# A transformer block on one core: the attention division is put ahead of the residual on VectorE, and the second norm's square root goes one slot later

## The chip, the cores and the metric

The kernel runs on one core of one Trainium2 chip. The metric is device time in microseconds (us): the median over runs of the whole program. All numbers of the profile come from one further execution, taken with the hardware profiler.

Five engines work side by side, each on its own list of instructions and strictly in the order of that list: TensorE (PE in the profile, its weight loads PEld), VectorE (DVE), ScalarE (ACT), GpSimd (POOL) and SyncE (SP), which here only issues DMA transfers. Engines wait for each other through semaphores.

## The reference

The input `x` is 4 sequences of 1024 tokens with 512 features, in float32; `t` is a condition vector for each sequence. What is computed:

```python
def _tc_rmsnorm(x, t, gw, gb, bw, bb):
    g = (t @ gw.T + gb)[:, None, :]
    b = (t @ bw.T + bb)[:, None, :]
    inv_rms = jax.lax.rsqrt(jnp.mean(x * x, axis=-1, keepdims=True) + EPS)
    return g * x * inv_rms + b

def _swiglu(x, gate_w, hid_w, out_w):
    return jax.nn.silu(x @ gate_w.T) * (x @ hid_w.T) @ out_w.T

def block(x, t, ...):
    x = x + attention(_tc_rmsnorm(x, t, g1w, g1b, b1w, b1b), Wq, Wk, Wv, Wo)
    return x + _swiglu(_tc_rmsnorm(x, t, g2w, g2b, b2w, b2b), gate_w, hid_w, out_w)

out = x + block(x, t, ...)
```

The attention has 16 heads of 32 features and a full softmax; the hidden size of the feed-forward part is 2048.

## The kernel before

**Tiling.** The 4096 tokens are 8 query blocks of 512 tokens (`n`). Activations lie transposed, features on the 128 partitions and tokens along the free axis. For each block, attention runs over 4 groups of 4 heads and 2 halves of 256 queries: 8 softmax jobs `j` for a block, 64 in all. A job takes 4 rounds `r`, each over 256 keys, so there are 256 rounds.

**Slots.** One loop, `while g < END`, runs a software pipeline over slots `g`, one round to a slot. The order on PE, DVE and ACT is the order in which the loop writes the instructions (`manual_schedule`); SP is ordered by the framework. In slot `g` the kernel computes the scores of round `g` (`scores`, L316, PE), copies them to SBUF (`keep`, L323, ACT) and takes them into the running maximum (`running_max`, L328, DVE); it adds the shift to round `g-5` (`shifted`, L369, DVE) and exponentiates it (`exponential`, L372, ACT); and it multiplies round `g-6` with the values (`weighted`, L382, PE). The exponential of one slot is therefore the operand of the `weighted` of the next. `kind = g % 4` tells the slots apart: in kind 0 the maximum of a finished job is transposed and split, and its sums are taken (`take_sums`); in kind 1 the shift is spread over the partitions (`parts_T`, `spread`) and `take_av` copies the finished product. Below, "slot 16" means the 16th slot of a block, `g % 32 == 16`; "third slots" are those with kind 2.

**Division.** `inverse` (L422, RECIPROCAL) and `normalize` (L431, a product) on DVE turn a job's product into attention output `oT`. They stand near the end of a kind 0 or a kind 2 slot: before slot `FS` = 60 in kind 2 (except for the last job of a block); from then on in kind 0, except for the jobs whose slot group starts at 12, 24 or 28 of a block, which go to kind 2, that is, to slots 14, 26 and 30.

**Feed-forward filler.** From slot 60 on, PE's free time is filled with the feed-forward part of the block before: one of 16 hidden tiles `p` for every two slots. The products `pa` and `pb` (L112) lie in PSUM. In an even slot: `pair_26`, `copy_156` (L545, ACT), `filler` (the contraction `pc` of an earlier tile with `ow`, 32 matmul records), `pair_7`, `sub_5` (L552, DVE, reads what `pair_7` wrote). The residual, `take_contract` (L583, DVE), adds `pc` to `res` and so sets the PSUM buffer of `pc` free. In an odd slot: `pair_3`, `gate_tanh` (L562, ACT), `pair_15` of the next tile, `take_5` (L526, ACT), `gate` (L567, DVE), `add_15` (L530, DVE), `pair_4`, `hidden` (L570, DVE). `pc` and `pa` share two PSUM buffers of the pool `ps`: the `pa` that `pair_15` opens in a kind 3 slot takes the buffer of the `pc` of the kind 2 slot ahead of it. Its first matmul (`pa<-x,fa`) waits for that residual.

**Second norm.** The scale of the feed-forward norm is made in small steps that are hung on the ends of slots (`after(g, ...)`; such work follows everything else in its slot): mean (`norm_mean`), `norm_compact` and `take` bring the 512 sums as a 128x4 tile `few` through DRAM, `root` (L173, ACT, a square root), `invert` (L177, DVE), `put` (L182, a DMA to DRAM) and `norm_spread` (L188, a DMA back, broadcast to 128 partitions). `norm_scale` (L199, DVE) then uses it. There are 7 of these chains in the loop, for blocks 0 to 6. `e` is `g0` for block 0 and `g0 - 4` for the others, where `g0 = (n + 1) * 32`.

**ACT's function tables.** The square root and the exponential need different tables; ahead of `root`, and again ahead of the next exponential, ACT gets an ACT_TABLE_LOAD (L173 and L372). Copies and the tanh need none of their own.

The even slots and the end of a slot before, where the change works (shortened):

```python
                one, two, evict = filler(p)
                one()
                two()
                if g < NR:
                    running_max(g, 0)
                    running_max(g, 1)
                if evict is not None:
                    evict()
                pair_7(p)
                sub_5(p)
```

Of the kernel before, what the change touches and what calls it, by code (L numbers as in the profile page):

```python
# [24 lines left out]
def tile_cond_transformer_block(  # L25
# [299 lines left out]
    def running_max(r: int, k: int):  # L325
        j, u = divmod(r, UN)
        if u:
            nc.vector.tensor_tensor(rmax[j], rmax[j], raw[r][:, k, :, :], ALU.max)  # L328
        elif k:
            rmax[j] = sb.tile([P, HG, HQ], F32, tag="rmax", name=f"rmax{j}")  # L330
            nc.vector.tensor_tensor(rmax[j], raw[r][:, 0, :, :], raw[r][:, 1, :, :], ALU.max)
# [74 lines left out]
    def take_av(j: int):  # L406
        avs[j] = sb.tile([P, HQ], F32, tag="avs", name=f"avs{j}", bufs=2)
        nc.scalar.copy(avs[j], av.pop(j))
# [12 lines left out]
    def inverse(j: int):  # L421
        nc.vector.reciprocal(state["total", j], state["total", j])  # L422
# [166 lines left out]
    GB = C * (NB // HQ)  # L589
    BS = GB * UN  # L590
# [15 lines left out]
    def after(g, fn, *a):  # L606
        ended.setdefault(g, []).append((fn, a))
# [21 lines left out]
    for b in range(1, B):  # L629
        for half in range(QB):  # L630
            s = math.ceil((len(queue) + 1) / PACE)
            s4 = s - 4 - (s - 6) % UN
            tag = f"a{b}_{half}"
# [10 lines left out]
    FS = BS + 28  # L644
# [3 lines left out]
    for n in range(NBLK):  # L648
        g0 = (n + 1) * BS
        pin(g0 + 6, load_res, n)  # L650
        e = g0 if n == 0 else g0 - 4
        go = e + 13 if n < NBLK - 1 else g0 + 8
        for d in range(C):
            first.append((go, None, project_out, (n, d)))
            pin(go - 3 + (d // 2 * 4 if n else 0), load_wo, n, d)
        if n < NBLK - 1:
            tag = f"f{n}"
            after(e + 16, add_res, n)
            for k in range(2):
                after(e + 15 + k, lambda n=n, tag=tag, k=k: norm_squares(x2[n], tag, k))  # L660
            if n == 0:
                between(e + 17, norm_mean, tag, False)
            else:
                amid.setdefault(e + 17, []).append((norm_mean, (tag, True)))
            after(e + 17, norm_compact, tag)
            after(e + 19, take, tag)
            after(e + 20, root, tag)
            after(e + (20 if n == 0 else 21), invert, tag)
            after(e + (21 if n == 0 else 22), put, tag)
            after(e + (22 if n == 0 else 24), norm_spread, tag)  # L670
            scales, mods = ((24, 24, 25, 25), (25, 25, 26, 26)) if n == 0 else ((22, 22, 24, 24), (23, 23, 25, 25))
            for c in range(C):
                after(g0 + scales[c], lambda n=n, tag=tag, c=c: norm_scale(x2[n], tag, c))
                between(g0 + mods[c], lambda n=n, c=c: norm_mod(1, n // QB, x2[n], c))
            for i in range(4):
                after(g0 + (26, 26, 27, 28)[i] - (n > 0 and i == 0), token_sums, n, i)
# [27 lines left out]
    with tc.manual_schedule(  # L704
# [69 lines left out]
        while g < END:  # L774
            kind = g % UN
            r_x, r_v = g - UN - 1, g - UN - 2
            x_on, v_on = 0 <= r_x < NR, 0 <= r_v < NR
            j_m = g // UN - 1
            m_on = 0 <= j_m < NR // UN
            j_s = g // UN - 2  # L780
            s_on = 0 <= j_s < NR // UN
            j_n = g // UN - 3
            n_on = 0 <= j_n < NR // UN
            ffn = g >= FS
            p = (g - FS) // 2
            even = g % 2 == 0
            columns[0] = DH

            if kind == 1 and m_on:
                parts_T(j_m)  # L790
            if g < NR:
                scores(g)
            if kind == 1 and m_on:
                spread(j_m, 0)
            if kind == 0 and n_on:
                fold_sum(j_n)
            if kind == 1 and j_n == GB + 1:
                normalize(GB)
            if x_on and kind != 1:
                shifted(r_x)  # L800
            if late is not None:
                late()
                late = None
            for fn, a in pinned.pop(g, []):
                fn(*a)
            if v_on:
                weighted(r_v)
                accumulate(r_v)
            if kind == 1 and m_on:
                spread(j_m, 2)  # L810
                mT.pop(j_m)
                shifted(r_x, slice(0, HG // 2))
                shifted(r_x, slice(HG // 2, HG))
            if g < NR:
                keep(g)
            if kind == 1 and s_on:
                take_av(j_s)
            due = bool(first) and first[0][0] <= g
            if not ffn:
                if x_on:  # L820
                    exponential(r_x)
                evict = chain(g, FG)
                if kind == 0:
                    take_sums(j_n)
# [3 lines that stand above are left out]
                if kind == 0 and m_on:  # L828
                    columns[0] = P
                    max_T(j_m)  # L830
                    parts(j_m)
                if evict is not None:
                    evict()
                for fn, a in halfway.pop(g, []):
                    fn(*a)
                if g == FS - 1:
                    columns[0] = DH
                    pair_15(0)
                    take_5(0)
                    add_15(0)  # L840
                elif even:
                    late = chain(g, FG)
                if g in (FS - 4, FS - 2):
                    load_f((g - FS + 4) // 2)
            elif even:
                load_f(p + 2)
                pair_26(p)
                copy_156(p)
                if kind == 0:
                    take_sums(j_n)  # L850
                if x_on:
                    exponential(r_x)
                if kind == 0 and m_on:
                    max_T(j_m)
                    parts(j_m)
# [3 lines that stand above are left out]
                if g < NR:  # L859
                    running_max(g, 0)  # L860
                    running_max(g, 1)
                if evict is not None:
                    evict()
                pair_7(p)
                sub_5(p)
                for fn, a in halfway.pop(g, []):
                    fn(*a)
            else:
                extra = due or len(queue) > FG
                evict = None  # L870
                if kind == 3 and extra:
                    evict = chain(g)
                pair_3(p)
                if kind == 3:
                    gate_tanh(p)
                if x_on:
                    exponential(r_x)
                pair_15(p + 1)
                take_5(p + 1)
                for fn, a in amid.pop(g, []):  # L880
                    fn(*a)
                if kind == 1:
                    gate_tanh(p)
                    if extra:
                        spare_bank[0] = True
                        evict = chain(g)
                if g < NR:
                    running_max(g, 0)
                if kind == 3 and evict is not None:
                    evict()  # L890
                if kind == 3:
                    gate(p)
                if g < NR:
                    running_max(g, 1)
                add_15(p + 1)
                if kind == 1:
                    gate(p)
                    if evict is not None:
                        evict()
                pair_4(p)  # L900
                hidden(p)
                if due:
                    chain(g)()
                for fn, a in halfway.pop(g, []):
                    fn(*a)
            if n_on and j_n < direct and kind in (0, 2):


                at = g - kind
                in_first = j_n % GB == GB - 1 or (at >= FS and at % BS not in (12, 24, 28))  # L910
                if in_first == (kind == 0):
                    inverse(j_n)

                    if j_n != GB:
                        normalize(j_n)
            columns[0] = DH
            for fn, a in ended.pop(g, []):
                fn(*a)
            if g == FS + 2 * FG - 2:
                load_ow(0)  # L920
            g += 1
# [90 lines left out]
```

## Time and profile before

| what | value |
|---|---|
| median of 3 runs | 2450.79 us (2449.7 to 2451.94) |
| the profiled execution | 2455.29 us, of which its span 2453.4 us |
| PE busy | 2385.5 us (97% of the span) |
| DVE busy | 1940.7 us (79%) |
| ACT busy | 1413.2 us (58%) |
| POOL busy | 172.4 us (7%) |
| mean granted TensorE clock | 0.994 |
| RECIPROCAL 128x256 (L422), 64 of them | 1744 ns each |
| product `oT` (L431), 64 | 425 ns |
| residual (L583), 128 | 689 ns |
| `sub_5` (L552), 128 | 430 ns |
| table load (L173, L372) | 1283 ns |

"Busy" is the time in which an engine had an instruction of the program running. The starts of records on one engine can lie closer together than their durations, since a next instruction may begin while the last one drains; for PE the ends are modelled. Where "waited for" is given, the profile infers the releaser from semaphore events. A time such as "974.22" is us from the start of the span. A slot is measured here from its first score matmul (L316) to that of the next.

### The profile page before, as it was taken

The page shows a single profiled execution, that of the slowest core. Times are in us where ns is not written, and L with a number is a line of the kernel's source. Part 1 is how long each engine was busy: PE and PEld are TensorE (multiplying, and loading weights), DVE is VectorE, ACT ScalarE, POOL GpSimd, SP SyncE. Part 2 cuts the span into 40 slices and gives each one's busy share as a digit, 9 for nine tenths or more (in the row PEclk, how much of TensorE's full clock was granted, in tenths as well). Part 3 has the DMA queues.
Part 4 walks back from the last instruction along what each step waited for, and adds up shares of the span by engine and source line. Part 5 has one row for each costly group of instructions (what it writes and reads, how often), then busy time and mean ns, then how long its engine had stood idle before and what let it go on. Part 6 is the DMA issues. An engine that isn't in the chain of part 4 may idle for free. (4 is left out here: it accounts for less than half of the span.)

```text
span 2453.4 us, 72677 instructions
## 1 busy us (share of the span) xinstructions
PE 2385.5 (97%) x32553; PEld 1135.9 (46%) x32553; DVE 1940.7 (79%) x2183; ACT 1413.2 (58%) x1495; POOL 172.4 (7%) x207
## 2 busy tenths in 40 slices
PE   8999999999999999999999999999999999999999
PEld 3333334344444544544454544454445445444444
DVE  2688888878799988998899979997999799843332
ACT  3677776765566656665566656665666566512110
POOL 0000000000000000000000000000000000000000
PEclk9999999999999999999999999999999999999999
DMA  6599999988788788889888888898788888853442
GB/s 216 166 304 259 256 258 240 231 202 219 198 205 210 188 226 209 208 207 229 204 200 213 225 197 209 204 230 207 198 207 203 224 200 204 198 165 117 140 131 70
DMA packets 185988, 501.79 MB, mean 205 GB/s; under 512 B 21319, under 2 KB 78663, under 8 KB 158286
## 3 DMA queue, kind: packets, MB, share of 16 engines
q0 software_dynamic: 28656, 208.68, 43.9%
q1 hardware_dynamic: 156734, 288.47, 35.4%
q8 instruction: 256, 4.19, 0.7%
q14 instruction: 54, 0.44, 0.1%
q10 hardware_dynamic: 288, 0.01, 0.0%
HBM read 246.44 MB, written 41.97 MB: 118 GB/s over the span
## 5 line engine op out<-in xcount | busy, mean ns | idle before, releaser
L369 DVE TENSOR_TENSOR raw<-raw,shift 128x2048 f32<-128x2048 f32 (+1 forms) x320 | 588.8, 1857 | 25.6 <-ACT shift L364 25.6
L323 ACT COPY raw<-sc 128x2048 f32<-128x2048 f32 x256 | 479.7, 1874 | 187.4 <-PE sc L316 130.8
L372 ACT ACTIVATE raw<-raw 128x2048 f32<-128x2048 f32 x256 | 490.8, 1917 | 157.1 <-DVE raw L369 154.8
L328 DVE TENSOR_TENSOR rmax<-rmax,raw 128x1024 f32<-128x1024 f32 x384 | 469.5, 1223 | 48.8 <-ACT raw L323 42.2
L112 PE MATMUL pc<-h,ow 128*32 128x512 f32 x4096 | 470.5, 596 | 5.2 <-DMA ow<-in_out_w 4.2
L382 PE MATMUL av<-raw,v 128*32 128x256 f32 x4096 | 271.9, 383 | 35.6 <-ACT raw L372 35.1
L396 POOL DMA_DIRECT2D raw<-raw x192 | 165.3, 861 | 1967.4 <-ACT raw L372 878.9
L316 PE MATMUL sc<-q,k 32*128 32x256 f32 x4096 | 293.3, 400 | 1.0 <-ACT raw L323 1.0
L112 PE MATMUL pa<-x,fa 128*32 128x256 f32 x4096 | 272.5, 384 | 4.1 <-DVE pa L530 4.1
L112 PE MATMUL pa<-sums,fw 128*32 128x256 f32 x4096 | 271.5, 383 | 0.0
L112 PEld LDWEIGHTS pc<-h,ow 128*32 128x32 f32 x4096 | 128.6, 110 | 250.7 <-issue 231.9
L316 PEld LDWEIGHTS sc<-q,k 32*128 32x128 f32 x4096 | 184.9, 184 | 117.4 <-issue 75.8
L112 PE MATMUL pkq<-y,wkq 128*32 128x512 f32 (+1 forms) x1664 | 232.5, 594 | 4.3 <-ACT y L202 4.1
L112 PEld LDWEIGHTS pa<-x,fa 128*32 128x32 f32 x4096 | 124.7, 110 | 119.7 <-DVE pa L530 21.4
L382 PEld LDWEIGHTS av<-raw,v 128*32 128x32 f32 x4096 | 110.4, 109 | 149.4 <-ACT raw L372 66.0
L112 PEld LDWEIGHTS pa<-sums,fw 128*32 128x32 f32 x4096 | 134.4, 111 | 90.0 <-issue 3.4
L583 DVE SCALAR_TENSOR_TENSOR res<-pc,res 128x512 f32<-128x512 f32 x128 | 88.2, 689 | 78.9 <-PE pc L112 76.2
L545 ACT COPY pb<-pa 128x256 f32<-128x256 f32 x128 | 46.1, 360 | 174.4 <-PE pa L112 173.3
L562 ACT ACTIVATE t<-pa 128x512 f32<-128x512 f32 x128 | 78.1, 610 | 109.9 <-PE pa L112 109.6
L112 PE MATMUL pb<-x,fw 128*32 128x256 f32 x2048 | 134.0, 379 | 1.2 <-ACT pb L545 1.2
L112 PE MATMUL pa<-x,fw 128*32 128x256 f32 x2048 | 134.0, 379 | 0.0
L552 DVE TENSOR_TENSOR pb<-pb,p 128x256 f32<-128x256 f32 x128 | 55.0, 430 | 99.8 <-PE pb L112 94.2
(108 smaller groups left out, 2243.7 us busy)
## 6 DMA issues: line engine op xcount, KB each, us to landing
raw<-raw POOLq DMA_DIRECT2D x192, 1024.0 KB, 9.3
fw<-sw SPq DMA_DIRECT2D x128, 512.0 KB, 7.8
fa<-in_gh_w SPq DMA_DIRECT2D x128, 384.0 KB, 6.8
ow<-in_out_w SPq DMA_DIRECT2D x128, 256.0 KB, 3.1
wkq<-in_kq_w SPq DMA_DIRECT2D x32, 512.0 KB, 6.2
v<-vs SPq DMA_DIRECT2D x128, 128.0 KB, 6.6
k<-kqs SPq DMA_DIRECT2D x124, 128.0 KB, 6.5
kqs<-st SPq DMA_DIRECT2D x61, 256.0 KB, 8.3
```

Source lines behind the costliest of these rows:

```text
L112: nc.tensor.matmul(dst[k : k + n, :], w[:, k : k + n], moving, start=start, stop=stop, skip_group_check=seeded)
L316: nc.tensor.matmul(sc[:, i, k, :], keys[rows, k * P : (k + 1) * P], queries[rows, :], start=True, stop=True)
L323: nc.scalar.copy(raw[r].rearrange("p k h q -> p h k q"), state.pop(("sc", r)))
L328: nc.vector.tensor_tensor(rmax[j], rmax[j], raw[r][:, k, :, :], ALU.max)
L369: nc.vector.tensor_tensor(t, t, s.unsqueeze(1).to_broadcast(list(t.shape)), ALU.add)
L372: nc.scalar.activation(raw[r], raw[r], AF.Exp)
L382: nc.tensor.matmul(av[j][i * DH : (i + 1) * DH, :], v[m, u][:, k, i * DH : (i + 1) * DH], raw[r][:, k, i, :], start=(kt == 0), stop=(kt == ...
L396: nc.gpsimd.dma_start(out=acc[j].rearrange("p k h q -> p (k h q)"), in_=raw[r].rearrange("p k h q -> p (k h q)"), accum_op=ALU.add,)
L545: nc.scalar.copy(bank_b[p][:, RIGHT], bank_a[p][:, RIGHT])
L552: nc.vector.tensor_tensor(b[:, LEFT], b[:, RIGHT], fifth.pop(p), ALU.subtract)
L562: nc.scalar.activation(state["t", p], bank_a[p], AF.Tanh, scale=0.5)
L583: nc.vector.scalar_tensor_tensor(r, pp, 0.5, r, ALU.mult, ALU.add)
```

## The change

Two things move. No instruction is added or removed.

First, the division. In the feed-forward stage its two instructions, where they belong to a kind 2 slot, are now written after the running maximum and before the residual (`evict`) and `sub_5`; before, they followed both. This concerns slot 62 (a slot whose `evict` is on ACT, so that only `sub_5` is passed) and 18 later slots: 14, 26 and 30 of six blocks. Kind 0 slots and slots before 60 keep the order they had.

Second, the norm's chain. `root` goes from the end of slot `e + 20` to that of `e + 21`, `invert` to `e + 22`, `put` stays at or goes to `e + 22`, `norm_spread` of block 0 goes one slot later. In the slots of a block: for six chains `root` goes from slot 16 to slot 17 and `invert` from 17 to 18; for block 0 `root` goes from slot 20 to 21 and `invert` from 20 to 22. On SP's list, `put` and `norm_spread` follow as neighbours: for six chains behind a load of `v` and one of `ow` that stood behind or between them, for block 0 behind two loads (`k`, `v`), three stores of `sv` and one more load of `k`.

```diff
-            after(e + 20, root, tag)
-            after(e + (20 if n == 0 else 21), invert, tag)
-            after(e + (21 if n == 0 else 22), put, tag)
-            after(e + (22 if n == 0 else 24), norm_spread, tag)
+            after(e + 21, root, tag)
+            after(e + 22, invert, tag)
+            after(e + 22, put, tag)
+            after(e + (23 if n == 0 else 24), norm_spread, tag)
...
+            def divide():
+
+                if n_on and j_n < direct and kind in (0, 2):
+                    at = g - kind
+                    in_first = j_n % GB == GB - 1 or (at >= FS and at % BS not in (12, 24, 28))
+                    if in_first == (kind == 0):
+                        inverse(j_n)
+
+                        if j_n != GB:
+                            normalize(j_n)
+
...
                if g < NR:
                     running_max(g, 0)
                     running_max(g, 1)
+                if kind == 2:
+                    divide()
                 if evict is not None:
                     evict()
                 pair_7(p)
...
-            if n_on and j_n < direct and kind in (0, 2):
-
-
-                at = g - kind
-                in_first = j_n % GB == GB - 1 or (at >= FS and at % BS not in (12, 24, 28))
-                if in_first == (kind == 0):
-                    inverse(j_n)
-
-                    if j_n != GB:
-                        normalize(j_n)
+            if kind == 0 or not ffn:
+                divide()
```

## The prediction, made before the result was known

> **What bounds the kernel now.** I first read the busy shares of the page: PE works 97% of the span, so the time falls only where PE stands still or is slowed. Next the view of waits for PE alone (who <- for whom: us in total, times, longest):
>
> ```profile
> PE av L382 <- ACT raw L372: 35.1, 37, 1.6
> PE pa L112 <- DVE pa L530: 4.1, 21, 0.2
> ```
>
> The first is half of what PE waits in all: `weighted` waits for the exponential of the slot before. Then I measured each slot from its first score matmul to the next and set slots with the same PE work side by side. In the feed-forward stage the same few stand out in every block: slot 18 takes 9.56 us where slot 30 takes 8.15; slot 16 takes 10.71 and slot 0 10.79 where slot 20 takes 9.91; slot 28 takes 12.60 or 13.65. Third, the timelines ahead of these slots, block `g0` = 96. ACT, slots 16 to 18 (start, duration):
>
> ```profile
> 964.08 1.91 ACT L372 ACTIVATE raw<-raw 128x2048 f32<-128x2048 f32 x1 [1.07 <-DVE raw L369]
> 966.00 1.28 ACT L173 ACT_TABLE_LOAD   x1
> 967.30 0.30 ACT L173 ACTIVATE fewf<-fewf,eps 128x4 f32<-128x4 f32 x1
> ...
> 973.51 1.28 ACT L372 ACT_TABLE_LOAD   x1
> 974.80 1.91 ACT L372 ACTIVATE raw<-raw 128x2048 f32<-128x2048 f32 x1
> ```
>
> The load to the root costs nothing (ACT idles 0.70 us after the root), but the load back stands at the end of slot 17, right ahead of an exponential for which PE waits in slot 18:
>
> ```profile
> 974.22 1.15 PE L316 MATMUL sc<-q,k 32*128 32x256 f32 x16
> 976.76 1.07 PE L382 MATMUL av<-raw,v 128*32 128x256 f32 x16 [1.39 <-ACT raw L372]
> ```
>
> DVE ahead of slot 16, then ahead of slot 28 in the same manner:
>
> ```profile
> 951.23 0.69 DVE L583 SCALAR_TENSOR_TENSOR res<-pc,res 128x512 f32<-128x512 f32 x1
> 952.16 0.43 DVE L552 TENSOR_TENSOR pb<-pb,p 128x256 f32<-128x256 f32 x1 [0.24 <-PE pb L112]
> 952.50 1.74 DVE L422 RECIPROCAL total<-total 128x256 f32<-128x256 f32 x1
> 954.28 0.43 DVE L431 TENSOR_TENSOR oT<-avs,total 128x256 f32<-128x256 f32 x1
> 954.62 2.28 DVE L369 TENSOR_TENSOR raw<-raw,shift 128x2048 f32<-128x2048 f32 x1
> ```
>
> ```profile
> 1043.35 0.68 DVE L583 SCALAR_TENSOR_TENSOR res<-pc,res 128x512 f32<-128x512 f32 x1
> 1043.95 0.42 DVE L552 TENSOR_TENSOR pb<-pb,p 128x256 f32<-128x256 f32 x1
> 1044.29 1.74 DVE L422 RECIPROCAL total<-total 128x256 f32<-128x256 f32 x1
> ```
>
> In slot 14 DVE waits for PE ahead of the residual and `sub_5`, and only then divides; the shift that follows makes the exponential late. In slot 26 no row has a wait: DVE is behind.
>
> **Root, part one of the sum.** In slot 17 nothing now lies between `avs` and the exponential. Slot 29, with the same work, starts it 5.17 us after the slot's start, and slot 30 takes 8.15 us. So slot 18 gives back 9.56 - 8.15 = 1.41 us. Block 0 is alike: slot 54 takes 10.46 us, slot 58 with the same 96 matmul records 9.05, again 1.41. Seven chains: 9.87 us.
>
> What the root meets at its new place: both loads now fall into slot 18 (54). I add ACT's rows from the slot's start, with slot 30 as the pattern: tanh ends at 1.83; load 1.28 and root 0.30 bring 3.44; copy of the scores 1.91, 5.35; `pb` 0.36, 5.71; load back 1.28, 7.0; exponential 1.91, 8.9. PE wants it in slot 19 at 8.15 + 1.07 = 9.22. Cover: 0.3 us (0.5 when rows overlap as they do now). The score copy ends at 5.35, DVE's maximum wants it at 5.46 (slot 30): just in time. `pair_7` at 7.17 wants `pb` at 5.71: hidden. If the cover is gone, each us past it costs 7 us. Bounds of this part: from 9.87 gained down to nothing gained, when a wait as long as the old one forms in slot 19. I take 9.87, since the sum is from rows of the same slots.
>
> The Trainium skill speaks against this ("ScalarE: Activation LUTs", What ACT_TABLE_LOAD costs): a switch of tables is a load of about 1283 ns and a drain of about 1380 ns, some 2.66 us together. The trace agrees on the load (1283 ns), but shows no drain: the load starts at 966.00, where the exponential ends (964.08 + 1.91), and the next activation starts 12 ns after it. By the page two drains would put the exponential 2.76 us later, at 11.7; PE would then wait 2.5 us instead of 1.4 and seven chains would lose about 7.5 us, an estimate.
>
> **Invert, put, spread.** `invert` (168 ns) leaves the stretch ahead of the shift in slot 18 for the end of that slot, DVE's work stays the same. `put` then waits on SP until about 983 less the gain; landing takes 3.2 to 4.9 us for `invs` and 3.9 for `totf` (view of these tiles), so the scale lies in SBUF near 991; `norm_scale` first needs it at 1014.1. Block 0: put about 488, spread landed by 497, needed at 503. Behind the two on SP stand loads of `q`, `v` and `fw` two or more slots ahead of their use; `v` and `ow` now go out before `put`'s wait. Cost 0, hidden by these 6 to 20 us.
>
> **Division, part two.** In slots with DVE behind, as slot 26, the start-to-start times are: maximum to next 1.14, RECIPROCAL 1.77, product 0.34, residual 0.60, `sub_5` 0.34. Together 4.19, against 4.74 in slot 14 (second maximum at 949.88 to shift at 954.62): 0.55 us of waiting. With the division first, PE's `pc` (its wait ended at 951.2) and `pb` (952.1) are long done when DVE comes to them, so the shift starts at 954.07. Slot 16 waits twice: 0.34 for the exponential (1.42 against 1.08), and about 0.4 for `add_15`, behind the same DVE work. 0.55 covers the first and half the second. Gain 0.55 in six blocks, 3.3 us; bounds 0 and the whole 0.80 (4.8 us). Slot 62 passes `sub_5` alone, which waits 0.42: its start-to-start sum is 3.59 against 4.10, gain 0.5 in slot 64. For slots 26 and 30 the sum stays 4.19: gain 0.
>
> What comes late: the residual, by 1.77 + 0.34 = 2.11 us, and with it PE's next `pa<-x,fa`, which takes its buffer; `sub_5` too, whose reader `pair_4` comes 1 us later still. Residual's end plus 0.05, against PE's start: slot 15, 953.87 against 954.78, hidden; slot 31, 1078.95 against 1079.23, hidden by 0.28; slot 27, 1046.20 against 1045.87: PE now waits 0.33 us there. But PE waits anyway a little later:
>
> ```profile
> 1045.87 1.05 PE L112 MATMUL pa<-x,fa 128*32 128x256 f32 x16
> ...
> 1051.29 1.07 PE L382 MATMUL av<-raw,v 128*32 128x256 f32 x16 [1.57 <-ACT raw L372]
> ```
>
> The shift and exponential behind this wait do not move, so the 0.33 comes off the 1.57. Cost 0; 2 us (6 x 0.33) if it is not taken up.
>
> **Clock, part three.** Stretches of 3.41 us that end where the granted clock changes (PE, PEld, DVE, ACT, POOL busy, clock, DMA):
>
> ```profile
> 1049.57:1052.98 3.41, 1.64 (x28) 0.71 (x28) 3.41 (x5) 3.41 (x3) 0.86 (x1) 1.00 0.90 296
> 1052.98:1056.39 3.41, 3.41 (x37) 1.49 (x28) 3.41 (x4) 0.64 (x2) 0.00 (x0) 0.50 1.06 270
> 1308.98:1312.39 3.41, 1.82 (x32) 0.91 (x36) 3.41 (x6) 3.37 (x3) 0.86 (x1) 1.00 0.73 263
> ```
>
> The first holds 1.77 us of idle PE in slot 28 (1.57 + 0.20), and the clock is halved in the next; the third, on the same grid, holds 1.59 and has no such sequel. Four of six blocks are hit, at 13.65 - 12.60 = 1.05 us each. With 0.33 moved to slot 27, at most 1.44 is left in any such stretch: four drops gone, 4.2 us. Bounds: 4.2 gained to 2.1 lost (all six hit). I take the gain, as stretches with 1.57 and 1.59 stayed at full clock.
>
> The Trainium skill ("TensorE: Matmul & The Clock Gate", the parts on the HAM clock gate and its oscillation) has the clock fall after an idle window of about 3.4 us. These rows show it after 1.77 us. By the page no gap here would count and the sum would lack the 4.2 us.
>
> **Sum.** 9.87 + 3.3 + 0.5 + 4.2 = 17.9 us. The profiled execution, 2455.29 us (span 2453.4 and 1.9 around it), would become 2437.4; the median of the runs lies 4.5 below it: 2450.79 - 17.9 = **2432.9 us**.
>
> **Rivals.** (A) Clock unchanged: the idle moves, but drops fall as often. For it: their grid does not follow the kernel. Against: the idle left is below every stretch that was followed by a drop. 2450.8 - 13.7 = 2437.1. (B) Only the root pays: the freed 0.55 us in slots 14 and 62 meets another wait, for instance the score copy that the maxima of slot 15 need (it ends at 955.03, the maximum would come at 956.27: against it), and the clock stays as it is. 2450.8 - 9.9 = 2440.9. (C) Slower: the stall goes from slot 18 to slot 19, because ACT's chain with both loads overruns its cover of 0.3 us. For it: the cover is thin. Against: every term is a measured row. It turns the total round once the new wait reaches about 1.8 us, where the half clock comes too: 7 x (1.8 + 1.05) = 20 lost against 17.9 gained. At a wait of 2.2: 7 x 3.25 - 17.9 = +4.9, 2455.7 us. (D) The change does nothing on the path, since other waits take up what is freed: 2450.8. Against: the gained slots have equals in the same trace that run without the stall.
>
> **How the numbers follow.** Forecast 0.58; A 0.20; B 0.11; D 0.05; C 0.06. A difference under 0.2% (4.9 us) counts as none. Faster 0.89, same 0.05, slower 0.06. Range: forecast with the whole wait of slot 16 (1.7 us more) and the scatter of the runs, 1.1 and some, 2428; at the other end B with that scatter, 2443. It leaves out C and D.
>
> **What would show it.** After: slot 18 at 8.15 us, with no wait for the exponential there or in slot 19; no table load between `avs` and the exponential of slot 17; slot 16 near 10.2; a wait of 0.3 us ahead of `pa<-x,fa` in slot 27 and slot 28 at about 12.3 in all blocks; no clock record of 0.5 in slot 28. It is wrong if slot 19 waits on ACT, if the shift of slot 15 starts no earlier, or if slot 27 waits over 1 us.

## The result and the profile after

| what | before | after |
|---|---|---|
| median of the runs (four each) | 2450.24 us (2448.89 to 2451.94) | 2435.15 us (2433.92 to 2436.16) |
| the profiled execution | 2455.29 us, span 2453.4 | 2435.25 us, span 2433.4 (one of the four) |
| mean granted TensorE clock of that execution | 0.994 | 0.998 |

The ratio is 0.994, with a 95% interval of 0.9928 to 0.9951: by the medians 15.1 us faster, by the interval 12.0 to 17.6. The forecast was 2432.9 us in a range of 2428 to 2443; it is 2.2 us too low. The two profiled executions differ by 20.0 us, five more than the medians. So two questions are left: whether each step did what was said of it, and what the odd microseconds are.

First the head of the page after, with the busy times. PE executes the same number of instructions; its busy time is lower by 6.6 us than the 2385.5 of before, which is mostly fewer half-clocked stretches.

```profile
span 2433.4 us, 72676 instructions
...
PE 2378.9 (98%) x32553; PEld 1131.6 (47%) x32553; DVE 1938.6 (80%) x2183; ACT 1412.7 (58%) x1495; POOL 172.4 (7%) x207
```

The view of waits for PE, after (who <- for whom: us in total, times, longest):

```profile
PE av L382 <- ACT raw L372: 21.1, 23, 1.6
...
PE pa L112 <- DVE pa L530: 2.7, 14, 0.2
...
PE pa L112 <- DVE res L583: 1.0, 6, 0.2
```

The wait for the exponential went from 35.1 us to 21.1, and 14 of its 37 occurrences are gone. The wait of the `pa` product for `add_15` lost seven of 21. The third line is new: six waits for the late residual, one in each block, as the prediction had for slot 27.

The timeline of ACT after, slot 17 into slot 18, block `g0` = 96:

```profile
962.47 0.39 ACT L408 COPY avs<-av 128x256 f32<-128x256 f32 x1
962.73 1.94 ACT L372 ACTIVATE raw<-raw 128x2048 f32<-128x2048 f32 x1
964.54 0.39 ACT L526 COPY p<-pa 128x256 f32<-128x256 f32 x1
964.79 0.63 ACT L562 ACTIVATE t<-pa 128x512 f32<-128x512 f32 x1
965.45 1.28 ACT L173 ACT_TABLE_LOAD   x1
966.74 0.30 ACT L173 ACTIVATE fewf<-fewf,eps 128x4 f32<-128x4 f32 x1
966.95 1.85 ACT L323 COPY raw<-sc 128x2048 f32<-128x2048 f32 x1
968.70 0.38 ACT L545 COPY pb<-pa 128x256 f32<-128x256 f32 x1
969.09 1.28 ACT L372 ACT_TABLE_LOAD   x1
970.38 1.92 ACT L372 ACTIVATE raw<-raw 128x2048 f32<-128x2048 f32 x1
```

The exponential of slot 17 now follows `avs` at once. Both table loads lie in slot 18, back to back with ACT's other work, and the exponential of that slot ends at 972.30. PE in the same two slots:

```profile
963.60 1.15 PE L316 MATMUL sc<-q,k 32*128 32x256 f32 x16
964.72 1.07 PE L382 MATMUL av<-raw,v 128*32 128x256 f32 x16
...
971.75 1.15 PE L316 MATMUL sc<-q,k 32*128 32x256 f32 x16
972.82 1.07 PE L382 MATMUL av<-raw,v 128*32 128x256 f32 x16
```

Neither `weighted` has a bracket, so neither waits: slot 18 runs from 963.60 to 971.75, 8.15 us, and slot 19 begins its product 0.52 us after the exponential is done. DVE ahead of slot 16, after:

```profile
940.94 1.75 DVE L422 RECIPROCAL total<-total 128x256 f32<-128x256 f32 x1
942.72 0.42 DVE L431 TENSOR_TENSOR oT<-avs,total 128x256 f32<-128x256 f32 x1
943.06 0.68 DVE L583 SCALAR_TENSOR_TENSOR res<-pc,res 128x512 f32<-128x512 f32 x1
943.66 0.42 DVE L552 TENSOR_TENSOR pb<-pb,p 128x256 f32<-128x256 f32 x1
944.00 2.28 DVE L369 TENSOR_TENSOR raw<-raw,shift 128x2048 f32<-128x2048 f32 x1
```

The waits of before (0.24 us in the bracket at `sub_5`, the rest ahead of the residual) are gone: the division fills that time. And PE in slots 27 and 28:

```profile
1034.18 1.07 PE L112 MATMUL pa<-x,fa 128*32 128x256 f32 x16 [0.16 <-DVE res L583]
...
1036.91 1.15 PE L316 MATMUL sc<-q,k 32*128 32x256 f32 x16
...
1039.25 1.07 PE L382 MATMUL av<-raw,v 128*32 128x256 f32 x16 [1.20 <-ACT raw L372]
```

The wait of 1.57 us in slot 28 has become 1.20. The length of the slots that the change touches (us, mean over their blocks; each block is within 0.02 unless two values stand there):

| slot | before | after | in all |
|---|---|---|---|
| 18, six blocks | 9.56 | 8.15 | -8.46 |
| 54, block 0 | 10.46 | 9.05 | -1.41 |
| 19 and 31 | 5.53 | 5.53 | 0 |
| 16, six blocks | 10.71 | 10.16 | -3.3 |
| 64 | 10.60 | 10.09 | -0.5 |
| 27, six blocks | 5.53 | 5.90 | +2.2 |
| 28, six blocks | 13.65 four times, 12.60 twice | 12.23 six times | -6.4 |

Together that is -17.9 us, the forecast's sum. The other 2 us between the two profiled executions come from two places that the change doesn't touch: slot 68 became 4.9 us shorter, and the tail, measured from the start of slot 255, became 3.0 us longer (342.70 to 345.72). Both are PE's waits for DMA transfers (the second by way of DVE's fold of the sums, L404), with a half-clocked stretch behind them when they are long:

```profile
592.47 2.78 PE L112 MATMUL pc<-h,ow 128*32 128x512 f32 x24 [2.08 <-DMA ow<-in_out_w]
...
2150.22 0.64 PE L414 MATMUL sum<-raw,ones_sum 128*32 128x256 f32 x8 [3.06 <-DVE raw L404]
```

The first wait was 4.21 us in the profile of before, the second 1.64. The experiments show how much these two vary without any change.

### The profile page after: what moved, and what is told of

Read it like the earlier page. It is cut to its first block, busy times and chain, and to the rows that moved or that the text cites. A ratio compares the mean times of both kernels' runs of the same rounds, so it can differ in the third digit from the quotient of the medians.

```text
span 2433.4 us, 72676 instructions
## 1 busy us (share of the span) xinstructions
PE 2378.9 (98%) x32553; PEld 1131.6 (47%) x32553; DVE 1938.6 (80%) x2183; ACT 1412.7 (58%) x1495; POOL 172.4 (7%) x207
## 3 DMA queue, kind: packets, MB, share of 16 engines
q8 instruction: 256, 4.19, 0.7%
## 5 line engine op out<-in xcount | busy, mean ns | idle before, releaser
L372 ACT ACTIVATE raw<-raw 128x2048 f32<-128x2048 f32 x256 | 491.0, 1918 | 149.8 <-DVE raw L369 147.3
L316 PE MATMUL sc<-q,k 32*128 32x256 f32 x4096 | 293.3, 400 | 1.1 <-ACT raw L323 1.1
L382 PE MATMUL av<-raw,v 128*32 128x256 f32 x4096 | 271.9, 383 | 21.6 <-ACT raw L372 21.1
L316 PEld LDWEIGHTS sc<-q,k 32*128 32x128 f32 x4096 | 184.9, 184 | 117.5 <-issue 74.9
L112 PEld LDWEIGHTS pa<-x,fa 128*32 128x32 f32 x4096 | 123.4, 109 | 120.7 <-DVE pa L530 21.1
L382 PEld LDWEIGHTS av<-raw,v 128*32 128x32 f32 x4096 | 110.4, 109 | 134.9 <-ACT raw L372 50.8
L112 PE MATMUL pb<-sums,fa 128*32 128x256 f32 x2048 | 133.9, 379 | 0.0
```

The costliest lines, as they stand in the source:

```text
L112: nc.tensor.matmul(dst[k : k + n, :], w[:, k : k + n], moving, start=start, stop=stop, skip_group_check=seeded)
L316: nc.tensor.matmul(sc[:, i, k, :], keys[rows, k * P : (k + 1) * P], queries[rows, :], start=True, stop=True)
L372: nc.scalar.activation(raw[r], raw[r], AF.Exp)
L382: nc.tensor.matmul(av[j][i * DH : (i + 1) * DH, :], v[m, u][:, k, i * DH : (i + 1) * DH], raw[r][:, k, i, :], start=(kt == 0), stop=(kt == ...
```

## The experiments

Each ratio is against the kernel before, run beside it on the same chip, with a 95% interval. The kernel before had medians of 2449.3 to 2450.2 us in these sets of runs; where a time is compared with the changed kernel's 2435.15, the two come from different sets.

### The two parts, each alone

`e1_root_only` is the kernel before with the second norm's chain moved; the division stays where it was.

```diff
-            after(e + 20, root, tag)
-            after(e + (20 if n == 0 else 21), invert, tag)
-            after(e + (21 if n == 0 else 22), put, tag)
-            after(e + (22 if n == 0 else 24), norm_spread, tag)
+            after(e + 21, root, tag)
+            after(e + 22, invert, tag)
+            after(e + 22, put, tag)
+            after(e + (23 if n == 0 else 24), norm_spread, tag)
```

> The kernel before with the later root, invert, put and spread alone; the division stays behind the residual. My theory: slots 54, 82, 114, 146, 178, 210 and 242 give back 1.41 us each, 9.9 us in all, and nothing else moves: slot 18 at 8.15 us, slot 16 still at 10.71, slot 28 still at 12.60 or 13.65. Ratio about 0.9960. Rival (the stall moves into slot 19): slot 19 over 5.6 us and a gain under 5 us.

Measured: 2439.76 us (5 runs), ratio 0.9959 (0.9946 to 0.9971), which is 10.0 us. Slot 18 takes 8.15 us and slot 54 9.05, slot 19 stays at 5.53. Slots 16, 27 and 28 are as before (one slot 16 of 11.05 us apart), with two of six blocks at 13.65 in slot 28.

`e2_division_only` is the opposite: the division is moved as in the change, the root stays at the end of slot 16.

```diff
-            after(e + 21, root, tag)
-            after(e + 22, invert, tag)
-            after(e + 22, put, tag)
-            after(e + (23 if n == 0 else 24), norm_spread, tag)
+            after(e + 20, root, tag)
+            after(e + (20 if n == 0 else 21), invert, tag)
+            after(e + (21 if n == 0 else 22), put, tag)
+            after(e + (22 if n == 0 else 24), norm_spread, tag)
```

(The lines with "-" are those of the changed kernel.)

> The kernel before with the earlier division alone. My theory: slot 16 loses 0.55 us in six blocks and slot 64 0.5, 3.8 us; slot 27 gains 0.37 and slot 28 loses it again, and no stretch of 3.41 us around slot 28 has over 1.5 us of idle PE, so that the halved clock in slot 28 is gone: up to 4.2 us more, 8.0 in all, ratio about 0.9967. Rival (the clock falls as often as before, or rarely fell in the runs without this profile): 3.8 us, ratio about 0.9985. Slot 18 stays at 9.56.

Measured: 2444.72 us (11 runs), ratio 0.9982 (0.9973 to 0.9991), which is 4.4 us. Slot 16 takes 10.16 us, slot 27 5.90 and slot 28 12.23 in all six blocks; slot 18 is back at 9.56. So the parts add up: 10.0 + 4.4 = 14.4, and both together gave 14.7 by the ratio, 15.1 by the medians. The root part is what its slots say (9.87). The division part is 4.4 (2.2 to 6.6 by its interval) where its own slots give 3.8. With the clock term at 4.2 it would have been 8.0, outside the interval. So the clock term is where to look.

### Where the clock's 4.2 us went

Slot 26's division alone decides whether the wait in slot 28 is 1.57 us or 1.20. `e3_slot26_behind` is the changed kernel with that one put back behind the residual, `e4_slot26_alone` the kernel before with that one alone moved.

```diff
-                if kind == 2:
+                if kind == 2 and g % BS != 26:
                     divide()
...
-            if kind == 0 or not ffn:
+            if kind == 0 or not ffn or g % BS == 26:
                 divide()
```

and, with the root back at the end of slot 16,

```diff
-                if kind == 2:
+                if kind == 2 and g % BS == 26:
                     divide()
...
-            if kind == 0 or not ffn:
+            if kind == 0 or not ffn or g % BS != 26:
                 divide()
```

> The changed kernel with the division of slot 26 put back behind the residual; slots 14, 30 and 62 and the root as changed. My theory: PE does not wait in slot 27 (5.53 us) and waits 1.57 us in slot 28 again, and wherever the 3.41 us grid falls so that 1.77 us of idle lie in one stretch the clock is halved after it, at 1.05 us each: 0 to 6.3 us slower than the changed kernel, about 4 when four of six blocks are hit, gain on before about 13.7 us. Rival (slot 26 has no part in the clock): same time as the changed kernel within 0.5 us, and no halved clock in slot 28.

> The kernel before with the division ahead of the residual in slot 26 alone; slots 14, 30 and 62 and the root as before. My theory: no instruction of DVE or ACT in slots 27 and 28 moves, PE waits 0.33 us in slot 27 and as much less in slot 28 (sum of the two unchanged), and what is gained is the halved clock alone: 0 to 6.3 us, 4.2 if four of six blocks are hit as in the profile of before. Rival: nothing, within 0.5 us. Slots 16 and 18 stay at 10.71 and 9.56.

Measured, `e3_slot26_behind`: 2436.09 us (5 runs), ratio 0.9949 (0.9936 to 0.9963). Slot 27 is back at 5.53; slot 28 takes 12.60 in five blocks and 13.65 in one. `e4_slot26_alone`: 2448.01 us (11 runs), ratio 0.9994 (0.9985 to 1.0002). Slot 27 takes 5.90 and slot 28 12.23 in all six; slots 16 and 18 are as before. The first kernel is 0.9 us slower than the changed one by the medians, the second 1.5 us faster than the kernel before. Both effects are too small to be told from none in the runs, and the second's interval ends at 3.7, below 4.2. The windows show why. Slot 28 in two blocks of `e3_slot26_behind` (window and its length, then busy time and instructions of PE, PEld, DVE, ACT and POOL, granted clock, DMA share, GB/s):

```profile
1037.20:1049.81 12.61, 10.40 (x134) 4.77 (x130) 12.14 (x17) 6.58 (x6) 0.88 (x2) 1.00 0.89 219
1293.29:1306.94 13.65, 11.88 (x135) 5.46 (x131) 12.22 (x17) 6.58 (x6) 0.90 (x2) 0.88 0.82 203
```

The same slot of the changed kernel:

```profile
1036.91:1049.14 12.23, 10.39 (x134) 4.76 (x131) 11.75 (x17) 6.58 (x6) 0.86 (x1) 1.00 0.83 215
```

At clock 1.00 slot 28 takes 12.60 with the 1.57 us wait and 12.23 without it; the 0.37 came back in slot 27. The clock is lowered in some blocks only, and not in all executions. To see how often, the kernel before was profiled once more as `e10_before_again`, with no edit.

> The kernel before once more, unchanged, for a second profile. My theory: the instructions' order in the slots is the same to 0.02 us, slot 28 is again 12.60 or 13.65, but how many of six blocks fall under the halved clock differs (4 in the first profile, 2 and 1 in the two others that keep this stall), and the waits for DMA in slot 68 and near the end differ by 1 to 3 us.

Measured: 2447.45 us (one run), span 2445.6, clock 0.998. From slot 13 on, all slots equal those of the first profile to within 0.02 us but slot 28, which takes 12.60 in all six blocks, and slot 68, 14.07 for 16.97. (Slots 11 and 12, ahead of the feed-forward stage, differ by 0.8 us in opposite directions.) One of its slots 28:

```profile
1044.67:1057.28 12.61, 10.40 (x135) 4.77 (x131) 12.13 (x17) 6.58 (x6) 0.86 (x1) 1.00 0.89 219
```

This block was a 13.65 of the first profile. So whether a block is hit differs from execution to execution of one and the same program. Counted over the profiles that keep the 1.57 us wait: four of six blocks before, two in `e1_root_only`, one in `e3_slot26_behind`, none in `e10_before_again`: 7 of 24, a mean of 1.75 hits and 1.75 x 1.05 = 1.8 us for one execution. In the seven profiles with the 1.20 us wait (after, `e2`, `e4`, both of `e5`, `e7`, `e8`) it is none of 42.

The traces also show which blocks are hit. Within each profile the stretches of lowered clock begin whole multiples of 3.413 us apart: before, at 793.57, 76 steps later at 1052.98, 227 steps further at 1827.80. Where this grid begins differs from execution to execution. In all seven hits a boundary of the grid lies 0.64 to 0.99 us behind the start of slot 28; in none of the other 17 blocks does one lie there (the nearest are at 0.54 and 1.08). Of the 42 blocks with the 1.20 us wait, 13 have a boundary between 0.64 and 0.99, and none is hit. Here are the stretch behind a boundary at 0.99 and the one after it, in `e3_slot26_behind` and then in the changed kernel:

```profile
1294.29:1297.70 3.41, 1.64 (x28) 0.70 (x28) 3.41 (x5) 3.41 (x3) 0.55 (x1) 1.00 0.80 234
1297.70:1301.11 3.41, 3.41 (x37) 1.52 (x28) 3.41 (x4) 0.64 (x2) 0.31 (x1) 0.50 1.10 317
```

```profile
1294.00:1297.41 3.41, 2.01 (x36) 0.95 (x36) 3.41 (x6) 3.33 (x3) 0.76 (x1) 1.00 0.70 254
1297.41:1300.83 3.42, 2.98 (x44) 1.61 (x39) 3.42 (x3) 0.73 (x2) 0.10 (x1) 1.00 1.12 302
```

With the grid at the same place PE idles 1.77 us in the first case and 1.40 in the second, and only the first is followed by the half clock. So the shorter wait does remove the drops, and where the wait is long, the place of the grid decides. The six blocks of one execution are not six draws: in `e3_slot26_behind` they lie about 256.07 us apart where 75 steps are 256.00, so that neighbours see nearly the same place. By an estimate, if every place of the grid is as likely as any other, the band (0.35 us wide at least, 0.54 at most, out of 3.41) makes 0.6 to 0.95 hits in six blocks, that is 0.7 to 1.0 us for an execution, less than the 1.8 that were counted.

### How much cover is left behind the new place of the root

Copies on ACT behind the root push the exponential of slot 18 back by an amount that the trace shows, to see where slot 19 begins to wait (rival C).

```diff
+        for _ in range(4):
+            nc.scalar.copy(few, few)
```

`e5_cover4` has four copies, `e5_cover1` one.

> The changed kernel with four copies of the 128x4 tile onto itself right behind the square root, on ACT, so that the exponential of slot 18 comes later by their time. The profile of the changed kernel leaves 0.47 us between the end of that exponential (8.71 us after the slot's start) and the product that needs it (9.23). My theory: what the copies take over 0.47 us is waited for by PE in slot 19 of six blocks; at 0.2 to 0.3 us a copy that is 0.3 to 0.7 us each, 2 to 4 us in all; block 0, with a cover over 1 us, loses nothing. Rival (ACT's chain is not what PE waits for there): no change, slot 19 stays at 5.53.

> As e5_cover4 with one copy. My theory: 0.2 to 0.3 us is inside the cover of 0.47: slot 19 stays at 5.53 us and no wait for ACT appears. Rival (the cover is the 0.3 us that was added up from rows, or less): a wait of up to 0.1 us in slot 19.

Measured with four: 2437.08 us (5 runs), ratio 0.9949 (0.9936 to 0.9961). The copies take 0.22 us each from start to start, and the exponential starts 0.91 us later in the slot (7.70 us after its start for 6.79). ACT, then PE, of that kernel around slot 19 (its lines behind the copies are numbered two higher, so L374 is L372, L318 is L316 and L384 is L382):

```profile
973.49 1.28 ACT L374 ACT_TABLE_LOAD   x1
974.79 1.91 ACT L374 ACTIVATE raw<-raw 128x2048 f32<-128x2048 f32 x1
```

```profile
975.24 1.15 PE L318 MATMUL sc<-q,k 32*128 32x256 f32 x16
976.75 1.07 PE L384 MATMUL av<-raw,v 128*32 128x256 f32 x16 [0.36 <-ACT raw L374]
```

The exponential ends at 976.70 and PE starts at 976.75, having waited 0.36: slot 19 takes 5.97 us for 5.53 in six blocks, and block 0 stays as it was. So 0.91 us of delay costs 0.44, and the cover is 0.47 us. With one copy (2437.97 us, one run) slot 19 stays at 5.53 us; what that run has more, it has in the tail, where the wait for the sums is 5.3 us long. The thin cover is real, but rival C's point of turning, a new wait of 1.8 us, would take a delay of 2.3 us.

### The two waits for transfers

`e7_ow_early` (the changed kernel with `ow`'s first load two slots earlier) asks whether slot 68's wait is only a late start of that load.

```diff
-            if g == FS + 2 * FG - 2:
+            if g == FS + 2 * FG - 4:
                 load_ow(0)
```

> The changed kernel with the first load of ow issued one pair of slots earlier (end of slot 64 in place of 66). My theory: the wait of PE for this load in slot 68 (2.08 us in the changed kernel's profile, 4.2 in that before, 2.6 to 2.9 in the others) comes from transfers queued around slot 67 and differs between executions; with the earlier issue it is gone, 2 to 3 us, and so is the halved clock there. Rival: the load waits for its buffer until the same time, nothing moves.

Measured: 2429.7 us (2429.1 to 2435.09, 5 runs), ratio 0.9921 (0.9907 to 0.9934), some 5 us below the changed kernel by the medians, though the two intervals just overlap. Slot 68 takes 9.91 us and waits for nothing. In the eleven profiles where the load starts at its old place this wait is 2.1 to 4.2 us, and the slot takes 13.6 us in the mean. So 3.7 us of the gain are seen in the slot; the rest is within the noise.

`e8_tail` asks the same of the tail. There the sums of the last job wait for three accumulating DMAs in a chain; DVE adds them instead.

```diff
+        elif j == NR // UN - 1:
+            nc.vector.tensor_tensor(acc[j], acc[j], raw[r], ALU.add)
         else:
             nc.gpsimd.dma_start(
```

> The changed kernel with the last softmax job's four exponentials added up on DVE in place of three accumulating DMAs. My theory: the wait of PE near the end (sum<-raw, 3.06 us in the changed kernel's profile, 1.64 in that before, 0.7 to 5.3 in the others) is for the last of three DMAs in a row, each waiting for the one ahead; with DVE, which is idle a good part of that stretch, it is gone, with the halved clock that follows it: 3 us off the median, slots 60 to 254 unchanged. Rival: DVE's three sums of about 2 us make gate or shift late there, no gain.

Measured: 2433.3 us (5 runs), ratio 0.993 (0.9916 to 0.9944); the interval overlaps the changed kernel's, so the gain, about 2 us where 3 were expected, is not certain. The trace is clearer. Here are DVE and PE in the tail of the kernel before, and the same matmuls of `e8_tail` (L416 is L414 there):

```profile
2170.42 1.23 DVE L404 TENSOR_TENSOR raw<-raw 128x1024 f32<-128x1024 f32 x1 [1.64 <-DMA raw<-raw]
2171.74 0.64 PE L414 MATMUL sum<-raw,ones_sum 128*32 128x256 f32 x8 [1.64 <-DVE raw L404]
```

```profile
2150.16 0.64 PE L416 MATMUL sum<-raw,ones_sum 128*32 128x256 f32 x8
```

The wait is gone, and the tail takes 341.4 us. Before, PE waits for DVE's fold of the sums (L404), which ends 0.1 us ahead of the matmul, and the fold itself had waited 1.64 us for the DMA chain, whose links land 8 to 14 us after their issue. With the chain, PE's wait was between 0.7 and 5.3 us over eleven profiles of kernels that are alike there; the two kernels with copies had 5.3 and 0.7. So the +3.0 us of the profiled pair is within what occurs without any edit to the tail. Whether the change lengthens this wait on the average stays open: waits over 3 us stand in four of the six profiles whose kernels have the later root and the earlier division of slots 14 and 30 together, and in none of the other five.

### Less DVE work ahead of the shift, and all together

What may be left in slots 0, 16 and 28 is the division as a whole, 2.1 us of DVE ahead of a shift. `e6_halves` takes it apart: for slots 26 and 30 half the reciprocal is done in the kind 0 slot before, for all three slots the product `oT` comes at the end of the kind 0 slot after, and one step of `token_sums` is moved within slot 28.

```diff
...
-                        inverse(j_n)
-
-                        if j_n != GB:
-                            normalize(j_n)
+                        if not ffn or in_first:
+                            inverse(j_n)
+                            if j_n != GB:
+                                normalize(j_n)
+                        elif at % BS == 12:
+                            inverse(j_n)
+                            after(at + 4, normalize, j_n)
+                        else:
+                            inverse(j_n, slice(P, HQ))
+                            after(at + 4, normalize, j_n)
+                    elif kind == 0 and at >= FS and at % BS in (24, 28):
+                        inverse(j_n, slice(0, P))
...
+                if i == 2 and n > 0:
+                    middle.setdefault(g0 + 28, []).append((token_sums, (n, i)))
+                    continue
```

> The changed kernel with DVE's work in slots 24 to 32 spread further: the first half of the reciprocal of slots 26 and 30 goes to the end of slots 24 and 28, their second half stays ahead of the residual, the products oT of slots 14, 26 and 30 go two slots later, and the third token sum goes from the end of slot 27 into slot 28, behind the split of the maximum. My theory (DVE's backlog sets slots 28, 0 and 16): slot 27 back to 5.53 us, slot 28 from 12.23 to about 10.8, slot 0 from 10.8 to about 9.9, slot 16 from 10.16 to about 10.0; some 2.8 us for each of six blocks, 15 to 17 us, ratio to before about 0.987. Rival (the moved parts make the shift of slots 25, 29 and 17 late): these slots grow by as much, gain under 5 us.

Measured: 2419.95 us (4 runs), ratio 0.9882 (0.9868 to 0.9895), about 15 us below the changed kernel. Slot 27 is back at 5.53 us, slot 28 takes 11.10, slots 0 and 16 take 9.91. Slot 28 of that kernel (L531 is L530 there):

```profile
1036.99 1.07 PE L382 MATMUL av<-raw,v 128*32 128x256 f32 x16 [0.26 <-ACT raw L372]
1038.26 1.07 PE L112 MATMUL pa<-x,fa 128*32 128x256 f32 x16 [0.20 <-DVE pa L531]
```

The wait of 1.20 us has come down to 0.26. Slot 28 stays 0.3 us above what was expected, since PE waits 0.36 for a residual at its end. The moved pieces were not tried one by one, so what each of them is worth is not shown.

`e9_best` is `e6_halves`, `e7_ow_early` and `e8_tail` in one kernel.

> e6_halves, e7_ow_early and e8_tail in one kernel. My theory: the parts are in different places and add up: about 15 us off the changed kernel for the halves, 3 for the load of ow, 3 for the tail, 2414 to 2418 us.

Measured: 2413.02 us (2412.06 to 2413.08, 4 runs), ratio 0.9849 (0.9835 to 0.9863): 37 us below the kernel before, 22 below the changed one and 1 below what was expected. Its page, and its largest wait of PE:

```profile
span 2411.2 us, 72705 instructions
...
PE 2372.8 (98%) x32553; PEld 1137.4 (47%) x32553; DVE 1940.4 (80%) x2199; ACT 1412.9 (59%) x1495; POOL 169.9 (7%) x204
```

```profile
PE av L382 <- ACT raw L372: 12.3, 17, 1.6
```

DVE works as long as in the changed kernel. What changed is only what stands ahead of each shift: PE's wait for the exponential went from 35.1 to 21.1 to 12.3 us.

## Why the prediction was right, and where it was off

**Root.** Right to the hundredth: 1.41 us in each of seven chains, 9.87 in all; alone it gave 10.0 in the runs (7.1 to 13.2 by the interval). Taking a slot with the same work and no stall (slot 30, slot 58) as the pattern for the slot to be cured was worth more than adding up instructions.

**Cover.** Forecast 0.3 us, or 0.5 if rows overlap as they did; measured 0.47. ACT's chain was laid out right: exponential ends 8.70 us after the slot's start where 8.9 was written without the overlaps. Slot 19 did not wait.

**No drain.** The load to the root starts at 965.45, within 0.03 us of the tanh's end (964.79 + 0.63), and the root 0.01 us after the load; the load back starts 0.01 us after `pb`. In these rows a switch costs 1.28 us and next to nothing more. (The tanh runs on the exponential's table: behind the square root of the tail it gets a load as well, at 2199.67, so its place ahead of `root` in slot 18 matters.) "ScalarE: Activation LUTs" (What ACT_TABLE_LOAD costs) in the Trainium skill adds a drain of about 1380 ns to each switch; no run here shows one. By an estimate from that figure slot 19 would have waited more than 2 us in the changed kernel, and it waited for nothing.

**Invert, put, spread.** Costed at nothing, and rightly: in `e1_root_only`, which moves them without the division, slots 18 and 54 gave back the whole of the root's term, so nothing of it went to them. One size was off. The landing of `totf`, priced at 3.9 us, takes 7.1 and 9.2 us in the two chains of the changed kernel for which the trace has it. In block 0 the load back is issued at 494.55 and `norm_scale` starts at 502.75 without a wait, so at 7.1 us some 1 us of cover was left there (an estimate), and not the 6 that were forecast.

**Division.** The second maximum to the shift of slot 14 takes 944.00 - 939.80 = 4.20 us; 4.19 was forecast. Slot 16 gave back 0.55 us, slot 64 0.51: 3.8 in all, as in the sum. The upper bound of 0.80 was not reached.

**Late residual.** Slot 31 and slot 15 take none of it, slot 27 does, and slot 28 gives it back: +0.37 and -0.37 us in all six blocks, with the clock at 1.00 in both. The forecast was 0.33. The bracket says 0.16, because records of matmuls that follow each other without a wait overlap (two in slot 27 start at 1035.07 and 1035.93 and last 1.05 each); the slot's length is the better measure.

**Clock.** The drops did go, as said, but the term was mis-sized. The step "Four of six blocks are hit, at 13.65 - 12.60 = 1.05 us each ... four drops gone, 4.2 us" took the count of one profiled execution as the count of every run. With the wait at 1.57 us blocks are hit 7 times in 24, so the term is 1.8 us in the mean, and 0.7 to 1.0 by the estimate from the grid. Then 13.7 and this make 14.4 to 15.5. Measured are 15.1, with an interval of 12.0 to 17.6, so the times alone can't tell these sums from 13.7 without any clock; that the drops went is shown by the profiles. The text itself had the warning: the profiled execution lay 4.5 us above the median, and its sum of 17.9 was taken off that median unchanged. The hits cost that execution at least 4.2 - 1.8 = 2.4 us more than the mean, and its wait in slot 68 was the longest of all profiles. A term that explains why the profile is slow can't be taken off a median that doesn't contain it. The gain was forecast 2.8 us too large; that the forecast time is 2.2 and not 2.8 us too low is luck, since the median of the kernel before fell by 0.55 with its fourth run.

**Rivals.** B (2440.9, only the root) fell with slot 16 at 10.16 and with `e2_division_only`. C (a stall in slot 19) fell with 5.53 us there; `e5_cover4` shows that the mechanism exists and where it begins. D fell with the medians. A (2437.1, drops as often as before) fell with 7 of 24 against 0 of 42, and, with the grid at the same place, 7 of 7 against 0 of 13. By size it did not fall: 2435.15 lies 1.95 us from A and 2.25 from the forecast.

## What to carry to other kernels

Set slots with the same work side by side: the one without a stall gives the price of the stall, and a list of start-to-start times says whether an instruction put ahead fills idle time or adds to the chain. Where a term comes from chance (a clock that falls in some blocks, a wait for a transfer), count it over several executions before taking it off a median, and look first at how far the profiled execution lies from that median. After a reorder has filled the idle time, the next gain is to move work out of the stretch altogether: the division taken apart, its pieces in slots that had room, brought as much again as the whole change.

## What the runs showed of the hardware that was not expected

The clock of the same slot, in the same program, is lowered in one execution and not in the next; in slot 28 the place of the grid of 3.41 us decided. A drop costs 1.05 us there (13.65 against 12.60), and it followed stretches of 3.41 us in which PE idled 1.77 us. "TensorE: Matmul & The Clock Gate" (the HAM clock gate) in the Trainium skill has the clock fall after an idle window of about 3.4 us; here just over half of that was enough. But idle time in one such stretch is not the whole rule: stretches with the same 1.77 us that began a little later in the slot (1.08 and 1.15 us after its start, against 0.64 to 0.99) were not followed by a drop, and neither were two with 2.0 us at slot 68, where two others with 1.9 and 2.0 were. What else decides stays open.

Transfers of one kind vary far more than the engines do. The wait for `ow` in slot 68 was 2.1 to 4.2 us where the load starts at its old place, and a chain of accumulating DMAs into one tile ended anywhere within 5 us. The slots' lengths, by contrast, repeated to 0.02 us from profile to profile, but for slots 10 to 12 and a few single ones such as the 11.05 above.
